# A two-layer convolution block on one core: a split-pool first seam, a second seam with its first image buffer in a pool of its own, and 32x32 products in the tail

## The chip, the core and the metric

The kernel runs on one core of one Trainium2 chip. A core has five engines that work side by side, each with its own queue of instructions: TensorE (PE in the profile, its weight loads PEld), VectorE (DVE), ScalarE (ACT), GpSimd (POOL) and SyncE (SP), which here only issues DMAs. The metric is the time of one execution on the device in microseconds (us). The kernel before takes 3523.01 us, the median of three runs (3522.52 to 3525.32).

## The reference: what is computed

The input x has 16 images of 192 channels and 64x64 pixels, all in float32. Two layers follow each other.

```python
h = _ln2d(x, ln1_w, ln1_b)                        # normalize over the channels
pg = _conv1x1(h, in_proj_w, in_proj_b)            # 192 -> 384 channels
projected, gate = jnp.split(pg, 2, axis=1)
projected = _dwconv3(projected, dw_k)             # 3x3, each channel by itself
scanned = _directional_scan(projected, ...)       # 4 decaying scans, mixed
local = _dwconv3(projected, le_k)
mixed = (scanned + local) * jax.nn.sigmoid(gate)
# batch norm over all images and pixels of a channel, then gelu
x = x + _conv1x1(gelu(bn(mixed)), out_proj_w, out_proj_b)
h2 = _ln2d(x, ln2_w, ln2_b)
x = x + fc2(gelu(fc1(h2)))                        # 192 -> 768 -> 192
# second layer, on the same 16 images
t = relu(scale(x.mean(axis=(2, 3)) @ w1.T))       # 48 numbers for each image
wt = (t @ w2.T + b2) * MASK                       # a 3x3 kernel for each image and channel
out = depthwise_conv(x, wt) + bias                # 4 of the 9 taps are left by the mask
```

The batch norm needs all images before any of them can go on, so the kernel has two seams at which one stage ends and the next begins.

## The kernel before, in words

The kernel has three stages. All orders of instructions are written out by hand (a manual schedule for all five engines): an engine executes its instructions in the order in which the program issues them, and waits for what each needs. Memory comes from pools; a new pool that lies where an old one lay waits for the old one's users.

**Projection** (the start and `project`, L553 to L571). The images are read in 64 chunks (`load_a`, four buffers `xa`). For each chunk, PE turns pixels to partitions (`turn`, L536, tiles xt), DVE takes the moments (`variance`, L543 and L544), ACT the root (`deviation`, L548), and PE multiplies by the weights `wi` (L565, tiles ps_pj). DVE and ACT evict with the scale (L570, L571) into one of two staging tiles: `stg`, or `mid` for odd blocks. Staging is stored to DRAM by groups of 8 channels (`store`, L598, tensors pg_d in five parts); group 0 is kept in SBUF (`store_first`, and for the last block `keep_first`, L591 and L593, after the last eviction). At the start, w_in is loaded into both halves of the partitions (`w0`, in the tile place), scaled by DVE (L310), averaged by PE (L314) and the mean subtracted (L317). Small preparations are hung beside given chunks (`beside`): the vectors from which the convolution matrices are built (loaded as dm and lm), the biases, and the load of the fc1 weights (wf1, wf in the profile) at chunk 62.

**Scans** (`depthwise` to `gate`). Channels are taken in 96 pairs, 4 pairs to a group of 8 channels. For a pair k PE does the 3x3 convolution as products with banded matrices (`depthwise`, L694, ps_d), ACT evicts it to q with three bias operations (L707, L709), DVE does two scans along rows of 1024 elements (L729, L731) with tables of decays made by ACT (L717), PE adds the local convolution (`local`) and the vertical scans (`vertical`), both L738 into ps_l, and DVE multiplies by the gate (L772) and takes the moments for batch norm (L774). The loop (from k=-2) issues vertical(k-1), gate(k-1), scans(k+1), depthwise(k+2), local(k), sigmoid(k). The groups' data arrive by `load_pg` (L681) into three buffers (pg_even, pg_o0, and the first part of mid), 4 MB each, on SP's queue; the products go back to DRAM (mixed_d, L786). Group 1 is loaded in two pieces: its first six images of eight on SP, the last two on POOL after the last block's stores. At k=0, PE also computes hidden_bias (L165) and squeeze_rows (L145); at k=1, 3, 5 ACT scales wf1 (`scale_hidden`, L171).

**The last stage** (`first`, L1080, to the end). After the moments (`class_sums`, `class_moments`, L800 to L808) and `batch_norm` (L812 to L817), images come back in 64 chunks of 512 pixels: DVE transposes (`turn_back`, L276), ACT GELU (`bn_gelu`, L953, L954), PE out projection (`out_proj`, L973 and L980), DVE residual (L986) into image buffers ximg, layer norm (`center` L1021, squares, roots L1046 and L1047), fc1 with GELU (`first`, L1080, L1082), fc2 (`seven`, L925), and onto the image. When a pair of images is complete, `squeeze` computes its taps (L1200 to L1208), and the dynamic convolution of that pair (`dynamic`, L1218 and L66) runs beside the next pair. `idle` and `keep_up` (recorded at L1293 and L823) issue products whose result is not used.

**The tail** (`dynamic_last`, after the loop). The last pair has nothing to run beside. Its 3 tiles of 64 channels (for two images: 128 partitions) have 64 rows each. DVE does tile 0 and 24 rows of tile 1 with four taps (the first on ACT, L1234, three on DVE, L66). PE does tile 2 and 40 rows of tile 1 with the taps on diagonals (`taps_on_diagonals`, L1428) in 64x64 products (L1246), which ACT evicts (L1248) and DMAs store (L1252).

The lines that the tail turns on:

```python
    first_o = room_for(0)
    for r in (0, CR):
        dynamic_last(last, r, CR, 0, None, first_o[:, r:r + CR])
        dynamic_last(last, r, CR, 2, dg2)
    dg1 = taps_on_diagonals(1)
    on_v(1, 1, 0)
    dynamic_last(last, GR, GR, 2, dg2)
```

## Time and profile before

| what | value |
|---|---|
| three runs, median (lowest to highest) | 3523.01 us (3522.52 to 3525.32) |
| the profiled execution, its own time | 3526.05 us |
| its span, first to last instruction | 3524.3 us, 78555 instructions |
| granted clock of PE, mean | 0.998 |
| busy, start (0 to 24 us): PE, DVE, ACT | 24.0 (modelled ends), 14.4, 8.6 us |
| busy, tail (3490 to 3525 us): PE, DVE, ACT | 24.1, 23.7, 14.4 us |
| DMA, whole span | 491.21 MB, mean 139 GB/s |
| DMA, 575 to 599 us | 340 to 418 GB/s in slices of 3 us |

A busy time says how long an engine had an instruction under way; the ends of PE's products are modelled, so that a busy PE is not PE at its peak. A row of the timeline gives the start, the length, the engine, the line, the operation, the tile written and the tile read with their shapes, how many instructions are merged in the row, and in brackets how long the engine sat idle before and what ended that. What ends an idle time is inferred; where the engine named had long been done it was another cause, often a DMA. The chain of waits is followed backward from the last instruction. "PE x128" counts records: each float32 product here has two.

### The profile page before, as it was taken

How to read it: one execution, taken by the hardware profiler on the slowest of the kernel's cores; microseconds unless marked ns; L12 is line 12 of the kernel's file. 1: busy time of each engine (PE TensorE's matmuls, PEld its weight loads, DVE VectorE, ACT ScalarE, POOL GpSimd, SP SyncE). 2: the span in 40 equal slices, each digit the busy share in tenths (PEclk: the TensorE clock that was granted, in tenths of full speed). 3: DMA queues.
4: the chain of work that ended last, by engine and by line, in shares of the span. 5: the costliest groups of instructions: out<-in, count | busy, mean ns of one | idle time of the engine just before them, and what ended most of it. 6: DMA issues, size and time to landing. Idle time of an engine off the chain costs nothing.

```text
span 3524.3 us, 78555 instructions
## 1 busy us (share of the span) xinstructions
PE 3500.5 (99%) x33148; PEld 1982.0 (56%) x33148; DVE 2741.1 (78%) x4666; ACT 1843.7 (52%) x2082; POOL 1177.1 (33%) x1322
## 2 busy tenths in 40 slices
PE   9999999999999999999999999999999999999998
PEld 7869996666666644444444444444444444444443
DVE  7888887999999965567777777777777777767766
ACT  4444446888888843435454544444444445454543
POOL 4545441111111043333343434333333333343433
PEclk9999999999999999999999999999999999999999
DMA  6999999999999941112232222222222222222213
GB/s 186 269 276 283 279 289 300 287 289 284 287 279 283 243 102 42 42 46 70 63 83 58 76 62 80 61 70 67 75 61 70 76 67 71 62 82 58 75 34 91
DMA packets 286505, 491.21 MB, mean 139 GB/s; under 512 B 24720, under 2 KB 180488, under 8 KB 286152
## 3 DMA queue, kind: packets, MB, share of 16 engines
q1 hardware_dynamic: 244100, 340.39, 35.5%
q0 software_dynamic: 41120, 144.77, 14.3%
q8 instruction: 261, 4.28, 0.5%
q10 hardware_dynamic: 932, 1.03, 0.1%
q14 instruction: 92, 0.75, 0.1%
HBM read 284.16 MB, written 197.92 MB: 137 GB/s over the span
## 4 chain that ended last, share of the span: by engine, by line
PE 96%; DVE 2%; DMA 1%; ACT 0%; issue 0%; SPq 0%; ACTq 0%; POOL 0%; DVEq 0%
PE ps_f L1080 28%; PE ps_f L925 19%; PE ps_pj L565 14%; PE ps_l L738 11%; PE ps_s L925 7%; PE ps_d L694 7%; PE ps_o L980 5%; PE ps_o L973 2%; PE ps_xt L536 1%; PE ps_m L1009 1%; PE ps_v L1009 1%; DMA dm<-dv_d 1%; DVE v L731 0%; DVE v L729 0%; DMA mixed_d<-mid 0%; DVE o L66 0%
## 5 line engine op out<-in xcount | busy, mean ns | idle before, releaser
L1080 PE MATMUL ps_f<-h,wf 64*64 64x512 f32 (+1 forms) x9240 | 1014.9, 589 | 0.0
L1082 ACT ACTIVATE gl<-ps_f,bf 128x1024 f32<-128x1024 f32 x384 | 428.2, 1115 | 1076.7 <-PE ps_f L1080 1076.4
L1080 PEld LDWEIGHTS ps_f<-h,wf 64*64 64x64 f32 x9240 | 347.1, 133 | 598.1 <-issue 573.2
L925 PE MATMUL ps_f<-gl,place 128*64 128x256 f32 (+1 forms) x3072 | 528.3, 486 | 1.1 <-ACT rs L1061 1.1
L565 PE MATMUL ps_pj<-wi,xa 64*128 64x384 f32 x3072 | 517.8, 485 | 0.7 <-ACT mid L571 0.4
L565 PEld LDWEIGHTS ps_pj<-wi,xa 64*128 64x128 f32 x3072 | 402.9, 187 | 79.9 <-DVE stg L570 1.7
L1115 POOL TENSOR_TENSOR gl<-gl 128x512 f32<-128x512 f32 x192 | 308.7, 1634 | 159.4 <-PE ps_f L925 159.4
L925 PEld LDWEIGHTS ps_f<-gl,place 128*64 128x64 f32 x3072 | 220.4, 137 | 222.5 <-issue 147.4
L1105 POOL COPY turn<-o 128x1 f32<-128x1 f32 x84 | 16.6, 197 | 820.9 <-DVE o L66 820.9
L1111 POOL TENSOR_TENSOR t<-gl 128x512 f32<-128x512 f32 x192 | 246.4, 1283 | 87.5 <-DVE low L276 44.2
L1113 POOL TENSOR_TENSOR t<-gl,t 128x512 f32<-128x512 f32 x192 | 247.5, 1289 | 43.6 <-ACT gl L1082 30.3
L66 DVE SCALAR_TENSOR_TENSOR o<-ximg,taps,o 128x1024 f32<-128x1024 f32 x180 | 231.7, 1288 | 4.9
L729 DVE TENSOR_TENSOR_SCAN v<-tab,q 128x1024 f32<-128x1024 f32 x96 | 218.3, 2274 | 5.6 <-ACT q L709 5.6
L731 DVE TENSOR_TENSOR_SCAN v<-tab,q 128x1024 f32<-128x1024 f32 x96 | 217.5, 2266 | 0.0
L1138 DVE SCALAR_TENSOR_TENSOR ximg<-ps_f,pt,ximg 128x256 f32<-128x256 f32 (+1 forms) x176 | 96.7, 549 | 145.5 <-PE ps_f L925 145.5
L717 ACT ACTIVATE tab<-mask,dec_b 128x1024 f32<-128x1024 f32 x192 | 209.7, 1145 | 0.1
L523 POOL DMA_DIRECT2D xa<-in_x_dram x201 | 126.1, 634 | 250.4 <-PE ps_pj L565 236.8
L571 ACT ACTIVATE stg<-ps_pj,rsa 128x384 f32<-128x384 f32 x128 | 120.3, 942 | 152.1 <-PE ps_pj L565 140.0
L571 ACT ACTIVATE mid<-ps_pj,rsa 128x384 f32<-128x384 f32 x128 | 119.8, 940 | 152.6 <-PE ps_pj L565 143.5
L986 DVE SCALAR_TENSOR_TENSOR ximg<-ps_o,pt,low 128x256 f32<-128x256 f32 x264 | 112.9, 479 | 94.6 <-PE ps_o L980 90.6
L980 PE MATMUL ps_o<-low,wo 128*64 128x256 f32 x1536 | 180.8, 384 | 1.8 <-ACT low L953 1.8
L276 DVE STREAM_TRANSPOSE low<-low 128x512 f32<-128x512 f32 x180 | 174.4, 1020 | 0.1
(279 smaller groups left out, 5669.8 us busy)
## 6 DMA issues: line engine op xcount, KB each, us to landing
low<-in_x_dram SPq DMA_DIRECT2D x128, 384.0 KB
out_dram<-o SPq DMA_DIRECT2D x172, 256.0 KB
mid<-pg_d SPq DMA_DIRECT2D x8, 4096.0 KB
low<-mixed_d SPq DMA_DIRECT2D x116, 256.0 KB
low<-pg_d SPq DMA_DIRECT2D x7, 4096.0 KB
pg_o<-pg_d SPq DMA_DIRECT2D x7, 4096.0 KB
xa<-in_x_dram POOLq DMA_DIRECT2D x201, 128.0 KB, 5.1
xa<-in_x_dram SPq DMA_DIRECT2D x183, 128.0 KB
```

The costliest lines, as they stand in the source:

```text
L66: nc.vector.scalar_tensor_tensor(o, in0, scalar, in1, ALU.mult, ALU.add, **kw)
L565: nc.tensor.matmul(ps[i], pixels(n, t, g)[q], wi[q, t].rearrange("p g k c -> p (g k c)"), start=(t == 0), stop=(t == 2))
L571: nc.scalar.activation(stag[blk][1][:, :, j], ps[1], AF.Copy, scale=rs[:, g, 1:2])
L694: nc.tensor.matmul(dst(ps[o, ih]), mats[g % 2]["dm"][q, di + 1, :, ch], src(s["pg"][q, :, 0, ch]), start=(di == 0), stop=stop)
L738: nc.tensor.matmul(dst(bst[k]["ps"][o, i]), lm_of(g)[q, m, :, c], src(q, ih), start=start, stop=stop)
L925: nc.tensor.matmul(ps[q], w(i), rhs(i), start=start, stop=stop, **kw)
L980: nc.tensor.matmul(ps[wh][q].rearrange("p (r w) -> p r w", w=32), wo[:, 64 * t:64 * t + 64], cols(rows(s["mx"][:, i]))[:, :, wh], start=fi ...
L1080: nc.tensor.matmul(pf[o, i, x], wf1[q, t, m0:m0 + 64], s["h"][q, t, x], start=(t == 0), stop=(t == 2))
L1082: nc.scalar.activation(gl, pf, AF.Gelu, bias=bf1[:, m:m + 1])
L1111: sub(t1[:, m], b12(m), b11(m))
L1113: sub(t2[:, m], b22(m), t1[:, m])
L1115: sub(b12(m), b22(m), b12(m))
```

## The change

The change has four places. Its parts, in the order of the program:

- **Start.** w_in is loaded into the lower half only, one DMA for each of three parts on SP's and ACT's queues; ACT writes the upper half of wi from it. Chunk 1 of x is loaded on both queues behind a copy of one pixel of chunk 0 (before: chunks 1 to 3 on POOL, behind a copy that needs all of chunk 0). The roots for chunk 0 are taken in two pairs, the reciprocals later.
- **First seam.** The pools are split and ordered so that pg_o0 and q lie over stg alone and ps_d over the banks of xt. The table of pair 0 is made beside chunks 53 and 55, in wf1's room; the idle products are gone; the last block's group 0 is copied in parts, the last rows from PSUM. depthwise(0) is done in two halves of the images, scans(0) in eight pieces. The order at pair 0 is other: depthwise(2) comes after vertical(0). dm(1) is loaded whole; dm(2) is loaded on POOL's queue; the last block's stores go image by image, and pg group 2 is loaded in two pieces.
- **Moved.** hidden_bias goes behind the second class's sums; its addition behind batch norm; squeeze_rows to pair 4; the load of wf1 to pair 88; scale_hidden to the last stage, between the two first GELUs.
- **Second seam.** The first image buffer gets a pool of its own; the first transpose goes between the two moments; the idle product has 256 columns; two transposes for chunk 1 go before the first residual.
- **Tail.** The squeeze of the last pair is done in three parts (tiles 0, 2, 1), with two idle products behind it. DVE does tile 0 only; PE does tiles 1 and 2 in 32x32 products (`dynamic_two`), ACT the first taps, the second diagonals and the evictions, with no DMA on ACT's queue.

The diff, cut to its core:

```diff
-                nc.vector.tensor_scalar_mul(wi[:, t], by_group(w0[:, t]), pt3[:, t, LN1W:LN1W + 1])
+                v, w = by_group(w0[lo, t]), pt3[lo, t, LN1W:LN1W + 1]
+                nc.vector.tensor_scalar_mul(wi[lo, t], v, w)
+                nc.scalar.activation(wi[HALF[1], t], v, AF.Copy, scale=w)
...
+            if n == 1:
+                for q in HALF:
+                    nc.gpsimd.tensor_copy(xa[q, :, 0:1], pixels(0, 1, AR - 1)[HALF[1], 127:128].unsqueeze(1).broadcast_to([64, 3, 1]))
...
+                if n == n_ac - 1 and g == AR - 1:
+                    keep_first(blk, slice(BR - AR, BR - 1))
+                if n == n_ac - 1 and g == AR - 1:
+                    for i, par, q, o in first_of(blk):
+                        if i == 0:
+                            nc.vector.tensor_scalar_mul(o[:, :, j], ps[0][q, 0:2 * GC], rs[q, g, 0:1])
+                        else:
+                            nc.scalar.activation(o[:, :, j], ps[1][q, 0:2 * GC], AF.Copy, scale=rs[q, g, 1:2])
...
-        for _ in range(3):
-            nc.tensor.matmul(warm_[:, 0:2 * C], ident, wi[:, 0].rearrange("p g k c -> p (g k c)"), start=True, stop=True)
-        keep_first(blk)
-        store(blk, 0, (nc.gpsimd, nc.gpsimd))
...
+            for im in (slice(0, n_half // 2), slice(n_half // 2, n_half)) if k == 0 else (slice(0, n_half),):
+                ps = psd.tile([128, 2, CH], F32, tag="d", name="ps_d", bufs=2)
...
         load_pg(1, nc.sync, 0, n_half - 2)
+        store(blk, 0, (nc.gpsimd, nc.sync))
         load_pg(1, nc.gpsimd, n_half - 2, n_half)
-        for d in range(1, len(PARTS)):
-            store(blk, d, (nc.sync, nc.sync))
-        load_pg(2)
+        for i in range(2):
+            for d in range(1, len(PARTS)):
+                store(blk, d, (nc.sync, nc.sync), (i,))
+        load_pg(2, nc.sync, 0, n_half - 2)
+        load_pg(2, nc.sync, n_half - 2, n_half)
...
-                    load_dm(g + 2)
+                    load_dm(g + 2, queues=(nc.gpsimd, nc.gpsimd) if g == 0 else (nc.sync, nc.gpsimd))
...
             if k == 0:
-                pb_h = psb.tile([128, 2, CH], F32, tag="d", name="pb_h", bufs=2)
-                hidden_bias(pb_h)
-                squeeze_rows(pb_h[:, 0, HCH:CH])
-                copy_dm(1)
-            if k in (1, 3, 5):
-                scale_hidden(k // 2)
+                vertical(0)
+                tables(2)
+                depthwise(2)
+            if k == 4:
+                squeeze_rows(psd.tile([128, 2, CH], F32, tag="d", name="pr_h", bufs=2)[:, 0])
+            if k == n_bp - 2 * hp_:
+                load_weights(1)
...
         class_moments(0, pt0)
+        turn_back(y_low, mxs[0], 0, 0)
         keep_up(1)
...
         class_moments(1, pt1)
+        pb_h = psl.tile([128, 2, CH], F32, tag="l", name="pb_h")
+        hidden_bias(pb_h)
         batch_norm()
-        turn_back(y_low, mxs[0], 0, 1)
+        v = bf1.rearrange("p (j i) -> p i j", i=2)
+        nc.vector.tensor_add(v, v, pb_h[:, :, 0:NPS])
         turn_back(y_low, mxs[0], 0, 2)
+        for t in range(2):
+            turn_back(y_low, mxs[1], 1, t)
...
-    slots = [k3.tile([128, 3, GR + 1, RW], F32, tag=f"ximg{i}", name=f"ximg{i}") for i in range(NSL - 2)] + late
+    k4 = ctx.enter_context(tc.tile_pool(name="k4", bufs=1))
+    slots = [(k3 if i else k4).tile([128, 3, GR + 1, RW], F32, tag=f"ximg{i}", name=f"ximg{i}") for i in range(NSL - 2)] + late
...
+        for k in range(NTAP):
+            for u, q in enumerate(QUAD):
+                for j, o in enumerate(QUAD):
+                    r0 = CR * (j % 2) + r + k // 3
+                    nc.tensor.matmul(rows(ps[u][o]), dg[q, k, q], slot(p, g + j // 2)[q, t, r0:r0 + nr, k % 3:k % 3 + HW],
+                                     start=(k == 0), stop=(k == NTAP - 1))
...
+    one(other_taps, 0)
+    dynamic_two(last, 0, 2, dg2, 0, CR // 2, False)
+    one(other_taps, 1)
+    dynamic_two(last, 0, 2, dg2, CR // 2, CR // 2, True)
     dg1 = taps_on_diagonals(1)
+    one(first_tap, 3)
+    one(other_taps, 2)
+    dynamic_two(last, 2, 2, dg2, 0, CR, False)
+    one(first_tap, 4)
+    one(other_taps, 3)
+    dynamic_two(last, 0, 1, dg1, 0, CR, True)
+    one(other_taps, 4)
+    dynamic_two(last, 2, 1, dg1, 0, CR, False)
```

In `dynamic_two`, u is the quarter of the partitions that a product reads (32 channels), j the quarter that it writes (8 or 4 rows of the image). For "apart" the results lie in four banks that ACT evicts one by one, otherwise in two pairs of banks.

## The prediction

> **What bounds the kernel now.** I read the page first, then the windows, then the chain of waits and the timeline at the places where the windows show TensorE short of work.
>
> ```profile
> PE 3500.5 (99%) x33148; PEld 1982.0 (56%) x33148; DVE 2741.1 (78%) x4666; ACT 1843.7 (52%) x2082; POOL 1177.1 (33%) x1322
> PE 96%; DVE 2%; DMA 1%; ACT 0%; issue 0%; SPq 0%; ACTq 0%; POOL 0%; DVEq 0%
> ```
>
> ```profile
> 24.00:560.00 536.00, 535.49 (x4494) 452.20 (x4492) 438.98 (x1344) 239.34 (x318) 234.38 (x443) 1.00 0.93 269
> 700.00:1200.00 500.00, 500.00 (x5813) 331.65 (x5809) 497.46 (x365) 424.00 (x508) 55.59 (x54) 1.00 1.06 284
> 1240.00:1270.00 30.00, 25.19 (x244) 14.23 (x242) 20.31 (x38) 13.67 (x18) 16.79 (x36) 1.00 0.57 146
> 1310.00:3440.00 2130.00, 2130.00 (x19456) 1003.40 (x19452) 1528.29 (x2613) 962.78 (x1000) 794.60 (x701) 1.00 0.24 64
> ```
>
> The columns of the second fence are the stretch, its length, then busy us of PE, PEld, DVE, ACT, POOL, the clock, the DMA share and GB/s. In the three long stretches PE is never short of work, and the change leaves the products there alone. What it touches are four short places: the start (0 to 24 us), the seam between projection and scans (568 to 625), the seam before the last stage (1240 to 1270), and the tail (3487 to 3524). Since PE is full in between, a microsecond won at a place comes out at the end, unless something later was waiting anyway.
>
> **The start: 1.5 us (0.5 to 2.5).**
>
> ```profile
> 1.57 6.34 DMA place<-in_w_in_dram
> ...
> 10.74 1.48 DVE wi L317 x3
> ```
>
> The chain of waits runs from the load of w_in (590 KB, both halves) to 7.91, through DVE's scaling, the mean product and the subtraction, to DVE's first statistics at 12.23; DVE is then the chain until 22.4. The change loads one half (295 KB) in three parts on two queues. At the 245 GB/s that the window from 4 to 6 us shows, 295 KB are 1.2 us; with less queued ahead of the pixels I take the landing at 6.2, 1.7 earlier. ACT makes the other half beside DVE: three copies of 384 elements, some 0.45 each (the 128x1536 square at L1029 takes 1.47 and the fixed part is small), done by 7.7, before the mean product. But the small load ptg is issued one ACT issue (0.7) later; it landed at 8.1, ACT waited 3.6 for it, and DVE's five gain operations (0.17 each) stand before the subtraction. That holds the subtraction to 9.2 or 9.9 instead of 10.74, a gain of 0.8 to 1.5. The reciprocals no longer wait for the root (0.37), and one more of 0.2 stands on the chain. Sum 1.5; ends from ptg late (0.5) to w_in at 5.5 and ptg early (2.5). The gate on one pixel replaces a copy of all (10.59), so x's second chunk starts earlier; behind the gate stand only the loads of later chunks, on POOL and SP.
>
> **The first seam: 3.8 us (2.4 to 6.9).**
>
> ```profile
> 568.73 2.20 PE L658 MATMUL pb<-wi,ident 128*128 128x384 f32 x6
> 569.82 0.84 ACT L593 ACTIVATE low<-mid 64x256 f32<-64x256 f32 x2
> 571.04 8.28 PE L694 MATMUL ps_d<-low,dm 64*64 64x512 f32 x116
> ...
> 575.96 2.29 DVE L729 TENSOR_TENSOR_SCAN v<-tab,q 128x1024 f32<-128x1024 f32 x1 [5.62 <-ACT q L709]
> 579.01 0.93 POOL L681 DMA_DIRECT2D pg_o<-pg_d  x1 [6.94 <-issue]
> ```
>
> ```profile
> 595.71 2.79 PE L694 MATMUL ps_d<-pg_o,dm 64*64 64x512 f32 x40
> ...
> 624.71 2.90 PE L694 MATMUL ps_d<-mid,dm 64*64 64x512 f32 x40 [1.26 <-DMA dm<-dv_d]
> ```
>
> PE fills 2.1 us with idle products until the copies of the last block end at 570.66. In the change the banks of ps_d are those of the pixel transposes, free since 560.9, and the first half of depthwise(0) needs only images 0 to 3, stored long ago: it starts at 568.8. Half a depthwise is ten groups of four products; 512+384+384 columns go at 0.4275 us per four of 512, and four of 120 took 0.119 (from the 2.61 of a whole one), so a half is some 1.5 us. The second half starts at 570.3; the last rows are copied by 569.3 (four POOL copies of 48 elements, COPY of one element 0.20, and small DVE and ACT copies from PSUM). DVE can scan the first half at 571.4 instead of 575.96; its eight short scans are a quarter of 2.27 each, and some 0.06 more. Following PE's new order (depthwise 0, 1, local 0, vertical 0, depthwise 2, 3, local 1, vertical 1) with 2.61 and 4.28 for depthwise and local+vertical, vertical(1) ends at 588.6 instead of 595.7: 7 us less. hidden_bias (2.17), the bias's wait (0.70), copy_dm (1.48 of ACT) and the table of pair 0 have left this stretch; the row product comes back at pair 4 for 0.46 of PE and 0.5 of DVE, which I count within it.
>
> The DMA takes some of it back. Depthwise(4) reads pg group 1, whose last quarter (1 MB, POOL) was issued at 579.01, when the last block's stores had landed, and landed 14.5 later at 593.5, 2.2 ahead of need. In the change two of these stores go on SP behind 3 MB of the group's head. SP waited for the stores from stg until 568.3, then for DVE and for the idle product until 571.0; now only for the first, and wf's 1.2 MB no longer run before it, against 0.4 MB more of dm. Head at 567, done at 576 to 579, the small stores behind it (waiting on SP for the last eviction, 569.8, with the sixteen large ones queued after them; these went at 571.5 before), the quarter issued at 578 to 581 and landed after 13.5 to 14.5: 591.5 to 595. So depthwise(4) starts near 593, a gain of 2.7 where 7 were free. Next is depthwise(8), which waited 1.26 until 624.58 for dm queued behind 4 MB on SP; dm goes to POOL's queue, and pg 2 no longer waits for all stores. 13.2 MB on SP from 567 at 350 to 380 GB/s, with 1.8 MB on POOL, end near 617, due at 593+27.6=620.6. Hence 624.7-620.6=4.1, less 0.3 for the row product: 3.8. With the quarter at 595 it is 2.4, with it in time 6.9. DVE and PE stand at 6.86 and 6.89 us a pair after that, so the lead is kept to the end of the stage.
>
> **The second seam: 1.6 us (0.5 to 2.2).**
>
> ```profile
> 1246.98 1.95 PE L1293 MATMUL ps_i<-wf,ident 128*128 128x512 f32 x4 [1.02 <-DVE mv L808]
> ...
> 1254.18 0.88 DVE L986 SCALAR_TENSOR_TENSOR ximg<-ps_o,pt,low 128x256 f32<-128x256 f32 x2 [3.83 <-PE ps_o L973]
> ```
>
> The chain of waits shows what the label of the last line hides: a store mixed_d<-mid from 1243.57 to 1253.94. The image buffer lies over mid; the product was done near 1252.4. A buffer elsewhere frees 1.8. The idle product of 256 columns is 0.55 shorter, and class_sums(1) follows it. One transpose (1.04) goes into DVE's wait of 1.67 between the moments; another follows the moments as before. So GELU starts at 1248.05 instead of 1249.46. Against it: hidden_bias (2.17 of PE) and its addition end at 1248.15, and the two idle products of the next pool may start only then and run 1.95, so the output product starts at 1250.15, not 1250.75. From there PE goes through without the wait of 1.12 for the residual; centering starts near 1258.4 instead of 1259.98. The three scalings of wf (0.93 each) now stand on ACT before GELU(1), until 1252.9; its last transpose ends at 1255.3, so they cost nothing; without this cover they cost 2.8. The load of wf at pair 88 lies 60 us ahead.
>
> **The tail: 3.2 us (-2 to 6).**
>
> ```profile
> 3490.72 8.59 PE L1246 MATMUL ps_d<-spare,low 64*64 64x256 f32 x96 [2.46 <-issue]
> 3499.12 13.92 PE L1246 MATMUL ps_d<-ximg,low 64*64 64x512 f32 x128
> ...
> 3514.23 1.11 ACT L1248 ACTIVATE ol<-ps_d,pt 128x1024 f32<-128x1024 f32 x1 [3.38 <-DMA out_dram<-ol]
> ...
> 3518.77 0.69 ACT L1248 ACTIVATE ol<-ps_d,pt 128x512 f32<-128x512 f32 x1 [3.42 <-issue]
> ```
>
> ```profile
> 3513.00:3518.00 5.00, 1.77 (x36) 0.97 (x27) 3.34 (x4) 1.11 (x1) 0.00 (x0) 0.96 0.87 259
> ```
>
> DVE's share falls from 88 to 64 rows (15.5 us at 3.88 per 16), PE's rises from 104 to 128, in five calls of 64 products of 32x32, 128 recorded pairs of load and product each, 640 in all. No 32x32 product is in this trace. Below, sixteen side by side would pass 512 columns in the time of four of 64x64: 0.4275/16, 26.7 ns a pair; above, if only four run together, 107 ns. In between, where the columns are few, a pair costs 30 (0.119/4), 33.5 (48 in 1.61 at L155) or 39 ns (24 transposes in 0.93). I take 33.5, the row with the fewest columns and narrow weights: 4.3 us a call. The split squeeze costs DVE 0.65, so PE starts at 3491.2 and ends at 3512.6; ACT needs 2.24 for the last two evictions; from the last eviction's end (3519.46) to the span's end were 4.84. That gives 3519.7. But the stores bind first: 3.15 MB stand behind 3510.6 at 0.298 MB per us (259 GB/s at a share of 0.87), so 3521.2, a gain of 3.2 with rounding. The stall of ACT on its own DMA issues, 3.4 us twice, goes with the scalar queue. Ends: 44 ns a pair gives 3526.3 (-2); 28 ns gives 3518.3 by the bytes (+6). The second idle product keeps the clock, which was 0.56 from 3490.7 to 3494.2; without it PE starts up to 1.7 later.
>
> [...]
>
> **Sum.** 1.5+3.8+1.6+3.2=10.1. The profiled execution has 3526.05 (span 3524.3 and 1.75 around it): 3515.95. The median of the runs is 3.04 below that: 3513.0.
>
> **Rivals.**
> - Forecast, all four near their values: 3513, chance 0.55.
> - The gains fall into other waits: pairs of 40 ns or more in the tail (for it: 39 ns at the transposes), the quarter of pg 1 at 595. 0.8+2.4+1.6+0=4.8, 3518; chance 0.22.
> - The DMA keeps up: pg 1 in time, stores smooth, 2.0+6.5+1.8+5=15.3, 3507.7; chance 0.15. Against it: shares of 1.0 from 575 to 600.
> - Slower: 32x32 products run only four at a time. N of 512 then costs 13.7 a call, 256 6.84: 54.7 instead of 21.4, and the kernel is at 3513.0+33.3, less the 1.5 of backlog that no longer counts: 3544.8. It decides from 40.6 ns a pair in the tail and from 51 ns for the whole kernel. Against it: 64x64 products do run four together here. Chance 0.08.
>
> A measurement tells some 0.2% (7 us) from no change. Faster by more: 0.55+0.15, same 0.22, slower 0.08. The range 3505 to 3521 adds the low ends (1.4) and the high ends (17.6) and leaves the slower rival out.
>
> **What would show it.** Start: first statistics near 10.7. First seam: depthwise at the last projection's end; a PE wait of some 4 us for pg_o near 589; none near 617. Second seam: no residual behind the store; ACT's three wf scalings between the GELUs. Tail: pairs near 33 ns; last DMA within 8 us of the last product. Wrong if PE's 32x32 groups of sixteen take over 0.8 us, or if pg 1 lands after 596.

## The result, and the profile after

The changed kernel takes 3520.07 us (median of 21 runs, 3516.17 to 3524.02), the kernel before 3525.87 beside it (21 runs, 3521.05 to 3533.96). The ratio is 0.9982 with a 95% interval of 0.9976 to 0.9987: **6.3 us faster (4.6 to 8.5)** by the ratio and 5.8 by the two medians, just under the 0.2% that I took as the bound of a difference. The forecast was 10.1 us. The profiled execution has a span of 3518.7 us (before 3524.3).

The busy times and the chain of the page, then the four stretches of the prediction:

```profile
PE 3496.4 (99%) x33570; PEld 1944.7 (55%) x33570; DVE 2736.0 (78%) x4669; ACT 1845.0 (52%) x2097; POOL 1184.1 (34%) x1338
PE 98%; DMA 1%; POOL 0%; SPq 0%; issue 0%; DVE 0%; ACT 0%; POOLq 0%; ACTq 0%
```

```profile
24.00:560.00 536.00, 534.51 (x4492) 358.67 (x4490) 439.77 (x1345) 241.31 (x321) 234.10 (x440) 1.00 0.95 270
700.00:1200.00 500.00, 500.00 (x5810) 380.05 (x5806) 497.47 (x364) 424.67 (x508) 54.95 (x53) 1.00 1.06 284
1240.00:1270.00 30.00, 28.92 (x262) 16.22 (x266) 17.25 (x35) 15.26 (x19) 15.77 (x34) 0.87 0.75 169
1310.00:3440.00 2130.00, 2128.85 (x19436) 1003.14 (x19430) 1529.29 (x2613) 963.96 (x1003) 794.86 (x703) 1.00 0.24 64
```

DVE has left the chain (2% before). The long stretches are as they were. The reader's eye should stop at the third row: PE is busier in the second seam (28.92 us for 25.19) and the clock is 0.87 where it was 1.00. More busy time at a lower clock is no gain.

Four distances split the two executions: to the end of the last gate, from there to the first product of the first fc1, from there to the reduction of the last pool (DVE's `pool<-sums`, the means that the last `squeeze` reads), and from there to the end of the span.

| us | before | after | gain | predicted |
|---|---|---|---|---|
| start and first seam: last gate's end | 1242.27 | 1236.11 | 6.16 | 1.5 + 3.8 |
| second seam: to the first fc1 product | 26.83 | 28.59 | -1.76 | 1.6 |
| last stage: to the pool's reduction | 2218.13 | 2218.13 | 0 | 0 |
| tail: to the end of the span | 37.07 | 35.87 | 1.20 | 3.2 |

**Start and first seam.** DVE's subtraction and first statistics; then the depthwise products, DVE's first scan, POOL's read of the last quarter, and the depthwise products of pairs 4 and 8:

```profile
9.62 1.48 DVE L319 TENSOR_TENSOR wi<-wi,pb 128x384 f32<-128x384 f32 x3 [1.08 <-PE pb L316]
11.02 0.36 DVE L558 BATCH_NORM_STATS2 st<-ps_xt 128x6 f32<-128x192 f32 x1
...
567.36 5.89 PE L724 MATMUL ps_d<-low,dm 64*64 64x256 f32 x114
570.46 4.77 DVE L762 TENSOR_TENSOR_SCAN v<-wf,q 128x256 f32<-128x256 f32 x8 [1.52 <-ACT q L740]
579.43 0.93 POOL L710 DMA_DIRECT2D pg_o<-pg_d  x1 [9.14 <-DMA pg_d<-mid]
590.39 2.91 PE L724 MATMUL ps_d<-pg_o,dm 64*64 64x512 f32 x40 [3.20 <-DMA pg_d<-mid]
618.69 2.80 PE L724 MATMUL ps_d<-mid,dm 64*64 64x512 f32 x40
```

The subtraction stood at 10.74 and depthwise(0) at 571.04. Now depthwise(0) follows the last projection at once, and the scan starts 5.5 us sooner. The bracket at 590.39 (pair 4) shows the new wait that the prediction named: 3.20 us for the last quarter. At pair 8 (618.69) the bracket is gone.

**Second seam.** The bias products (`hidden_bias`, L165, 36 records of one column), the idle pair (L1358, two products whose result is not used), the first output product and the first residual:

```profile
1239.87 4.00 PE L165 MATMUL pb_h<-pt,wf 64*128 64x1 f32 x36
1244.14 3.78 PE L1358 MATMUL ps_i<-place,ident 128*128 128x512 f32 x4 [0.27 <-DVE bf L921]
1247.85 1.12 PE L1024 MATMUL ps_o<-low,wo 128*64 128x256 f32 x8
1249.63 0.88 DVE L1030 SCALAR_TENSOR_TENSOR ximg<-ps_o,pt,low 128x256 f32<-128x256 f32 x2 [2.33 <-PE ps_o L1017]
```

The bias products took 2.17 us in before, where they stood in the first seam:

```profile
582.03 2.17 PE L165 MATMUL pb_h<-pt,wf 64*128 64x1 f32 x36
```

The idle pair took 1.95. Here the two take 4.00 and 3.78. Cut where the granted clock changes, the windows show why (columns as in the prediction, the clock is the third number from the end):

```profile
1234.31:1237.72 3.41, 3.41 (x43) 3.02 (x40) 3.38 (x6) 2.00 (x3) 1.33 (x3) 1.00 0.05 10
1237.72:1241.14 3.42, 3.42 (x28) 3.40 (x30) 2.47 (x8) 0.28 (x1) 0.89 (x1) 0.50 0.79 197
1241.14:1244.55 3.41, 3.14 (x27) 3.06 (x28) 1.50 (x7) 2.53 (x3) 0.00 (x0) 0.50 1.04 296
1244.55:1247.96 3.41, 3.41 (x6) 0.87 (x7) 2.75 (x3) 2.50 (x4) 0.03 (x1) 0.50 0.46 136
```

PE has half the clock for 10.24 us, three stretches of 3.41. Note that PE is "busy" all that time: neither PE's busy time nor a wait in brackets gives it away.

**Tail.** The products of 32x32 squares, the last evictions, and the windows to the end:

```profile
3487.04 4.12 PE L1305 MATMUL ps_d<-spare,low 32*32 32x256 f32 x198 [1.27 <-DVE low L1501]
...
3497.92 4.75 PE L1305 MATMUL ps_d<-spare,low 32*32 32x512 f32 x112
...
3505.64 2.30 PE L1305 MATMUL ps_d<-ximg,low 32*32 32x512 f32 x59 [0.31 <-issue]
3507.89 2.12 ACT L1314 ACTIVATE ol<-ps_d,pt 128x1024 f32<-128x1024 f32 x2 [2.68 <-issue]
```

```profile
3508.00:3511.00 3.00, 0.00 (x0) 0.00 (x0) 0.00 (x0) 2.02 (x2) 1.59 (x3) 1.00 0.91 295
3511.00:3514.00 3.00, 0.00 (x0) 0.00 (x0) 0.00 (x0) 0.00 (x0) 0.54 (x1) 0.50 0.95 253
3514.00:3516.00 2.00, 0.00 (x0) 0.00 (x0) 0.00 (x0) 0.00 (x0) 0.00 (x0) 0.50 0.88 282
3516.00:3518.70 2.70, 0.00 (x0) 0.00 (x0) 0.00 (x0) 0.00 (x0) 0.00 (x0) 0.50 0.17 57
```

198 records in 4.12 us are 20.8 ns a pair of load and product at 256 columns; 112 in 4.75 are 42 at 512. The last eviction ends at 3510.01, 9.4 us sooner than before's (3519.46) on the clock of the span and 5.0 sooner behind the pool's reduction (27.2 us for 32.2), but 8.7 us pass from there to the end, where before had 4.84.

### The profile page after: what moved, and what is told of

It reads as the page before. It is cut to its first block, busy times and chain, and to the rows that moved or that the text cites. A ratio compares the mean times of both kernels' runs of the same rounds, so it can differ in the third digit from the quotient of the medians.

```text
span 3518.7 us, 79438 instructions
## 1 busy us (share of the span) xinstructions
PE 3496.4 (99%) x33570; PEld 1944.7 (55%) x33570; DVE 2736.0 (78%) x4669; ACT 1845.0 (52%) x2097; POOL 1184.1 (34%) x1338
## 4 chain that ended last, share of the span: by engine, by line
PE 98%; DMA 1%; POOL 0%; SPq 0%; issue 0%; DVE 0%; ACT 0%; POOLq 0%; ACTq 0%
PE ps_f L1124 28%; PE ps_f L969 19%; PE ps_pj L580 14%; PE ps_l L768 12%; PE ps_s L969 7%; PE ps_d L724 7%; PE ps_o L1024 5%; PE ps_o L1017 2%; PE ps_xt L551 1%; PE ps_m L1053 1%; PE ps_v L1053 1%; PE ps_d L1305 0%; DMA xa<-in_x_dram 0%; POOL xa L538 0%; SPq L623 0%; DMA pg_d<-mid 0%
## 5 line engine op out<-in xcount | busy, mean ns | idle before, releaser
L762 DVE TENSOR_TENSOR_SCAN v<-tab,q 128x1024 f32<-128x1024 f32 x190 | 423.4, 2270 | 0.3 <-ACT q L740 0.3
L580 PEld LDWEIGHTS ps_pj<-wi,xa 64*128 64x128 f32 x3072 | 308.0, 187 | 170.1 <-DVE stg L593 3.0
L558 DVE BATCH_NORM_STATS2 st<-ps_xt 128x6 f32<-128x192 f32 x512 | 172.1, 336 | 2.8 <-PE ps_xt L551 2.7
```

What stands on the lines that cost most here:

```text
L580: nc.tensor.matmul(ps[i], pixels(n, t, g)[q], wi[q, t].rearrange("p g k c -> p (g k c)"), start=(t == 0), stop=(t == 2))
L762: nc.vector.tensor_tensor_scan(v_, t_, q_, 0.0, ALU.mult, ALU.add)
```

## The experiments

A median of these kernels is sure to some 3 us: all ratios to before below lie between 0.9970 and 0.9987 with intervals that overlap. So the verdicts rest on the distances inside the profiles. Three of them, in us, with the number of 3.41 us stretches at half clock in brackets:

| kernel | depthwise(0) to last gate's end | to the first fc1 product | pool to the end | ratio to before |
|---|---|---|---|---|
| before | 671.2 [1] | 26.83 [0] | 37.07 | 1 |
| e11_before | 670.7 [2] | 28.53 [2] | 37.29 | - |
| after | 668.8 [0] | 28.59 [3] | 35.87 | 0.9982 (0.9976 to 0.9987) |
| e1_idle512 | 670.3 [1] | 27.84 [2] | 34.20 | 0.9983 (0.9975 to 0.9992) |
| e2_hb_early | 673.0 [2] | 24.60 [0] | 35.82 | 0.9987 (0.9978 to 0.9995) |
| e3_stores_pool | 670.5 [1] | 26.04 [1] | 36.11 | 0.9986 (0.9978 to 0.9995) |
| e4_tail_before | 669.1 [1] | 25.96 [1] | 37.30 | 0.9986 (0.9977 to 0.9995) |
| e5_wide_fill | 669.7 [0] | 27.85 [2] | 34.85 | 0.9978 (0.9969 to 0.9986) |
| e6_fewer_bytes | 667.7 [0] | 28.72 [3] | 34.54 | 0.9970 (0.9957 to 0.9983) |
| e7_one_pool | 669.9 [1] | 28.60 [3] | 34.52 | 0.9971 (0.9959 to 0.9982) |
| e8_split_last | 668.7 [0] | 28.59 [3] | 36.35 | 0.9985 (0.9976 to 0.9994) |
| e9_bias_spread | 674.1 [1] | 25.39 [2] | 34.84 | 0.9986 (0.9977 to 0.9995) |
| e10_all | 670.0 [0] | 24.30 [0] | 38.24 | 0.9983 (0.9974 to 0.9991) |
| e12_quiet | 671.3 [2] | 26.25 [1] | 34.37 | - |

In after, e3, e4, e6, e7, e8 and e12 the second seam is the same code (but for e7's pool), and it takes 26.0 to 28.7 us.

### The idle product of 512 columns again

```
-                nc.tensor.matmul(ps[:, 0, 0:HCH], ident, place[:, 0:HCH], start=True, stop=True)
+                nc.tensor.matmul(ps[:, 0], ident, place[:, 0:CH], start=True, stop=True)
```

> The changed kernel with one edit: the idle product at the second seam has 512 columns again (on the small block that the change gave it). In the changed kernel's trace the granted clock falls to 0.50 between 1237.9 and 1247.9 us, after the idle product of 256 columns (0.68 us), while in the trace of before, with 512 columns (1.10 us), it stays at 1.00; the bias products, the two idle products behind them and the way to the first output product then take about 3.5 us more than at the full clock (4.00 for 2.17, 3.78 for 1.95). Theory A, the shorter idle product lets the clock fall: the clock stays at 1.00 through the seam, the bias products take about 2.2 us and the idle pair 1.95, the first output product comes about 9.5 us behind the last gate (12.9 in the changed kernel), and the kernel is 3 to 3.5 us faster than the changed one (about 3517, ratio to before near 0.9973). Rival B, the fall comes from where the stretch of short products lies or from what follows it (the bias products of one column): the clock falls again, the time is that of the changed kernel within 1 us (ratio 0.9982).

The clock fell all the same, 5 us later, for two stretches:

```profile
1236.05:1239.46 3.41, 3.41 (x37) 2.73 (x32) 3.31 (x7) 2.00 (x3) 1.64 (x3) 1.00 0.05 12
1239.46:1242.87 3.41, 3.41 (x49) 3.27 (x48) 2.68 (x6) 0.72 (x2) 0.56 (x1) 1.00 0.87 220
1242.87:1246.29 3.42, 3.16 (x12) 1.83 (x12) 3.01 (x9) 3.16 (x4) 0.00 (x0) 0.50 1.06 302
```

The stretch of the 512 columns kept the clock, the next, with the bias products, lost it. Theory A falls as the only cause. That the bias products bring it down holds for this run; it does not hold for after, where the clock was gone at 1237.72, 2 us before the first of them. What is left of the rival there is where the stretch of short products lies.

### The bias products early

```
+            if k == n_bp - 2:
+                pb_h = psd.tile([128, 2, CH], F32, tag="d", name="pb_h", bufs=2)
+                hidden_bias(pb_h)
...
-        hidden_bias(pb_h)
         batch_norm()
```

> The changed kernel with the 36 bias products and their addition taken out of the second seam and put into the scan stage, behind the last but one channel pair's local products; the idle product keeps its 256 columns. Theory A (the clock falls before the bias products begin, by the short products of the moments and the 256 columns): the clock falls to 0.50 at the same place, the idle pair takes 3.8 us but starts about 4.2 us sooner, the first output product comes at about its earliest, 9.5 us behind the last gate, 3.4 less than in the changed kernel; of this about 2.2 are paid in the scan stage, where PE has no free time, so 1 to 1.5 us faster than the changed kernel (ratio to before near 0.9978). Rival B (the bias products of one column bring the clock down): the clock stays at 1.00 in the seam and the idle pair takes 1.95; the time is the same as under A, the clock tells them apart.

The seam kept its clock with the 256 columns and was the shortest so far, 24.60 us. The clock fell where the bias products had gone, in the middle of the scan stage:

```profile
1226.92:1230.33 3.41, 3.41 (x52) 2.58 (x48) 3.40 (x3) 3.41 (x4) 0.00 (x0) 1.00 0.28 88
1230.33:1233.74 3.41, 3.41 (x20) 1.11 (x20) 2.31 (x3) 1.18 (x2) 0.00 (x0) 0.50 0.32 93
```

Rival B, in this one profile: the bias products at one place bring the clock down, even between local products of 512 columns. They cost 3.1 us there (650.45 us from the products behind the first seam's wait to the last gate, 647.4 in the kernels without them and with the same stretch lost in the first seam), 2.2 of their own; that the rest is the clock's is my reading.

### The small stores on POOL's queue

```
-        store(blk, 0, (nc.gpsimd, nc.sync))
+        store(blk, 0, (nc.gpsimd, nc.gpsimd))
```

> The changed kernel with the small stores of the first seam on POOL's queue alone; in the changed kernel half of them go by SP's queue, behind the large read of the odd rows, and POOL's read of the last quarter waits 9.14 us for them (issued at 579.43, landed near 590.2), so that the depthwise products of the fifth pair wait 3.20 us. Theory A, the order in the queue holds them up: the quarter is issued at 574 to 576, the wait at the depthwise products shrinks to under 1 us, and the kernel is 2 to 3 us faster than the changed one (ratio to before 0.9974 to 0.9976). Rival B, the DMA engines are full in this stretch, so that the quarter lands as late wherever it is queued: wait and time stay within 0.7 us of the changed kernel's.

```profile
576.76 0.93 POOL L710 DMA_DIRECT2D pg_o<-pg_d  x1 [6.43 <-DMA pg_o<-pg_d]
589.41 3.35 PE L724 MATMUL ps_d<-pg_o,dm 64*64 64x512 f32 x28 [3.20 <-DMA pg_d<-mid]
```

POOL's read of the quarter was issued at 576.76, 2.67 us sooner than in after (579.43), of which 0.97 is the earlier start of depthwise(0): 1.70 sooner behind it. TensorE's wait stayed at 3.20 us and ended 23.02 us behind depthwise(0) (23.03 in after). The DMA engines were at 0.92 to 1.09 of their time from 567 to 591 us in both. So rival B, as far as one profile each can tell: in the other kernels with after's queues and the same products in the seam, that wait ended between 21.4 and 24.0 us behind depthwise(0).

### The tail of before

The functions of before's last stage in place of the new ones (the taps in one piece, squares of 64x64, all diagonals on VectorE).

> The changed kernel with the last stage's end of the kernel before: the taps of the last pair in one piece, the products of 64 by 64 squares, no further idle products, all diagonals on VectorE. It gives what the new tail is worth. Theory A, what the two traces show from the reduction of the pool to the end of the span (37.07 us before, 35.87 after): the kernel is 1.2 us slower than the changed one (ratio to before near 0.9986). Rival B, my predicted 3.2 us, of which something else hid 2 in the profiled execution: 3 us slower (ratio 0.9991). Rival C, the clock of 0.56 that the kernel before had in its tail for 3.5 us costs more than the new products gain: no difference.

37.30 us from the pool to the end, as in both profiles of before (37.07, 37.29). The new tail took 34.2 to 36.1 in the seven kernels that have it unchanged and whole, 35.2 in the mean. It is worth 2 us, more than the first pair of profiles shows and less than predicted. The ratio can't tell the three theories apart.

### Wide idle products at both seams

```
+                if k == hp_:
+                    for _ in range(3):
+                        nc.tensor.matmul(ps[:, 0], ident, wide, start=True, stop=True)
...
+            if m % 4 == 0:
+                nc.tensor.matmul(pb[:, 0, HCH:CH], ident, place[:, 0:HCH], start=True, stop=True)
...
-        keep_up(1)
+        keep_up(2)
...
-    idle(2)
+    idle(1)
```

The bias products are 18 products in 36 records, so the edit put two idle products between them, not three.

> The changed kernel with wide idle products where its stages meet. First seam: three of 512 columns on the idle TensorE in front of the fifth pair's depthwise products (the wait there is 1.9 to 3.2 us). Second seam: two of 256 columns for one behind the first moments, one of 256 in front of every 12 of the 36 bias products, and one of 512 for two behind them, so that the seam has about as many wide columns as before, but spread. Theory A, the clock falls for a whole number of stretches of 3.41 us when too few wide columns fall into such a stretch, wherever it begins in that run: the granted clock stays at 1.00 in both seams; from the depthwise products behind the wait to the last gate 645.7 us (647.4 in the runs with a fall there), from the last gate's end to the first product of the first fc1 about 25.5 us (28.6, 27.8, 26.0 and 26.0 in the runs with three, two, one and one stretch), and the kernel is about 2.5 to 3.5 us faster than the changed one (ratio to before 0.9972 to 0.9976). Rival B, the bias products of one column bring it down whatever lies between them: the clock falls in the second seam still, and the gain is at most the first seam's 1.7 us. Rival C, the idle products are themselves on the path and cost what the clock gives: ratio as the changed kernel's, 0.9982.

The first seam kept its clock, but the products stood on the path for what the clock gave back: 669.7 us is no better than the others. In the second seam the clock fell twice, once from the stretch with the products of 48 columns (L155) and once from the one with the bias products and two wide ones:

```profile
1233.55:1236.96 3.41, 3.41 (x51) 3.30 (x48) 3.38 (x6) 2.00 (x3) 1.11 (x3) 1.00 0.02 4
...
1240.37:1243.79 3.42, 3.42 (x40) 2.66 (x40) 2.21 (x8) 2.57 (x3) 0.00 (x0) 1.00 1.03 291
1243.79:1247.20 3.41, 3.15 (x9) 1.26 (x10) 3.05 (x4) 2.06 (x4) 0.07 (x1) 0.50 0.53 155
```

Rival C in the first seam; in the second the clock fell with wide products between the bias products, as B has it. Its ratio's interval includes the changed kernel's ratio.

### Fewer bytes at the end

```
+                if t == 1 and g == 0:
+                    continue
```

> The changed kernel without the eight stores (128 KB each, 1.05 MB of the last pair's 6.29 MB) of the last but one call of the last stage's products; that part of the output is left out. Theory A, the bytes bind the end (the DMA engines are at 0.88 to 0.95 of their time from 3502 to 3516 us, at some 280 GB/s): the last 1.05 MB goes, the end comes sooner by 1.05 MB over 280 GB/s, 3.7 us, as far as the last eviction lets it: from the last eviction's end to the end of the span 5 to 6 us instead of 8.7, from the reduction of the pool to the end 32 to 33 us instead of 34.2 to 36.1. Rival B, what stands behind the last eviction is the time of the last stores themselves (32 partitions each, 4.4 us from issue to landing at the median): the tail stays at 35 us or above.

34.54 us, where A wanted 32 to 33; 7.05 us from the last eviction to the end, where A wanted 5 to 6. A sixth of the bytes (not a twelfth, as the text of e8 below has it), 3.7 us of transfer, brought 0.6 against the mean of 35.2. The way out did get shorter, 7.05 us for 8.6 to 10.4 in the seven kernels with the whole tail (9.2 in the mean), but the last eviction ended later, 27.5 us behind the pool for 25.2 to 27.2 (26.0 in the mean). So the bytes are a part of the way out, and not the bound of the tail alone. A wait grew: TensorE stood for 1.41 us in front of its last products (0.31 in after) and waited for nothing that the profile shows:

```profile
3504.27 2.30 PE L1305 MATMUL ps_d<-ximg,low 32*32 32x512 f32 x59 [1.41 <-issue]
```

### The image buffers in one pool again

```
-    slots = [(k3 if i else k4).tile(...
+    slots = [k3.tile(...
```

> The changed kernel with the image buffers in one pool again, so that the first residual's target lies with the rest. My prediction counted 1.1 to 1.6 us for the second seam, most of it since the residual no longer stands behind the last stores of the scan stage. Theory A, the pool of its own lets the first residual go sooner: the first residual waits for a store of the scan stage in this kernel, and the way from the last gate's end to the first fc1 product is longer by 1 to 2 us at the same number of stretches at half clock (27 to 28 us at one stretch, for 26.0). Rival B, the first output product comes too late for the residual to wait for a store at all (9.1 us and more behind the last gate's end where the clock falls): no difference beyond the stretches at half clock.

28.60 us at three stretches, as 28.59 in after. The first residual started 1.81 us behind the first output product (1.78 in after), and waited for that product. Rival B: the pool of its own is worth nothing in this order of work. Elsewhere it may be worth something: in e10 and e2, whose bias products are out of the seam and whose clock held, the first residual started at 1246.96 and 1249.07, before the scan stage's store that POOL issued landed (1248.27 and 1250.07). Neither was run with one pool. The ratio of 0.9971 comes from six runs and its interval touches the changed kernel's; nothing in its profile makes it faster, so I don't take it for a better version.

### The last call in two

```
-    dynamic_two(last, 2, 1, dg1, 0, CR, False)
+    dynamic_two(last, 2, 1, dg1, 0, CR // 2, False)
+    dynamic_two(last, 2, 1, dg1, CR // 2, CR // 2, True)
```

> The changed kernel with the last call of the last stage's products cut in two calls of 256 columns a square (the first into a pair of banks, the second into four banks apart); the same products and bytes. In the changed kernel 8.7 us pass from the end of the last eviction (1024 columns a partition, 128 KB in each of its four stores) to the end of the span, where before had 4.8, and leaving out a twelfth of the bytes a call earlier brought it to 7.0 only. Theory A, what the last eviction has left to store sets the end: the last eviction ends about as early, with half as much behind it, so 6 to 7 us to the end, and from the reduction of the pool to the end 33 to 34 us (34.2 to 36.1 in the runs so far). Rival B, the DMA engines work off a queue that is full since 3502 us, so that the size of the last piece doesn't matter: 34.2 to 36.1. Rival C, smaller pieces are stored at a lower rate (256 columns are 1 KB a row): slower than 36.

Half right: 6.5 us from the last eviction's end to the end of the span instead of 8.7. But the whole tail took 36.35 us, where the seven kernels with one call took 34.2 to 36.1: rival C's number, though the way out did not get slower. TensorE now stood still twice:

```profile
3503.89 2.79 PE L1305 MATMUL ps_d<-ximg,low 32*32 32x256 f32 x128 [1.25 <-issue]
3509.55 1.62 PE L1305 MATMUL ps_d<-ximg,low 32*32 32x256 f32 x59 [2.87 <-issue]
```

"issue" says that the profile shows nothing that held it. In the DMA records, packets of 16 KB of the queue "instruction" ran from 3501.51 to 3502.43 and from 3507.33 to 3508.29; TensorE went on 1.46 and 1.26 us behind them.

### The bias products spread

```
+            if n_bp - 6 < k < n_bp - 2:
+                m = 2 * (k - n_bp + 5)
+                pb_h = psd.tile([128, 2, CH], F32, tag="d", name="pb_h", bufs=2)
+                hidden_bias(pb_h, (m,))
+                nc.scalar.activation(hb_s[:, m:m + 2], pb_h[:, :, m // 2], AF.Copy)
```

> The changed kernel with the bias products taken out of the second seam and spread over the scan stage, 6 of the 18 behind each of the local products of three of the last pairs, copied by ScalarE and added in the seam. In the runs so far every stretch of 3.41 us at the full clock with 40 or more weight loads and under about 2100 columns (of the whole array) was followed by half clock, and none with 32 loads or fewer; the bias products at one place brought the clock down even in the scan stage, between products of 512 columns. Theory A, it is their density: spread, no stretch of the scan stage falls to half clock, the stage pays about 2.2 us (their time on PE), and from the last gate's end to the first fc1 product it is 24.6 us as with the bias products away altogether; of the two sums (from the depthwise products behind the wait to the first fc1 product) about 672.5 to 674 us, where the changed kernel's seam gave 671.7 at one stretch and 674.3 at three, both without a fall in the first seam. Rival B, any such product does: the clock falls in the scan stage still, 674 to 676.

The scan stage kept its clock with the same products, 12 records to a pair, in this profile and in e10's: it is their density (theory A), as far as two profiles with them spread and one with them together (e2) show. They cost 2.7 us there (650.1 us from the products behind the wait to the last gate, 647.4 with a stretch lost in the first seam and no bias products). The sum that theory A put at 672.5 to 674 us is 675.5 (650.1 and 25.4), the rival's number, but by the second seam: it lost the clock all the same, from a stretch with 40 records of L155:

```profile
1239.08:1242.49 3.41, 3.41 (x50) 3.10 (x46) 3.38 (x6) 2.00 (x3) 1.26 (x3) 1.00 0.06 14
1242.49:1245.91 3.42, 2.46 (x17) 2.28 (x16) 2.31 (x8) 0.05 (x1) 0.95 (x1) 0.50 0.75 193
```

### Three edits together

> Three edits together: the bias products spread as in the run before this, the idle product of 512 columns at the second seam, the last call of the last stage in two. If their effects add up, 1 to 2 us from the second seam and 1 to 2 from the end: about 3 us faster than the changed kernel, ratio to before 0.997 to 0.9975. Rival: the seam's gain is paid in the scan stage and the end is bound by its bytes, ratio 0.998 as the changed kernel.

The one execution whose clock held at 1.00 from 5 us to the end of the products; its second seam is the shortest, 24.30 us. Yet the ratio of 0.9983 is the rival's: 2.9 us were paid in the scan stage, and in the tail TensorE waited 1.40 and 3.40 us for "issue" (38.24 us):

```profile
3503.02 2.81 PE L1308 MATMUL ps_d<-ximg,low 32*32 32x256 f32 x128 [1.40 <-issue]
3509.24 1.46 PE L1308 MATMUL ps_d<-ximg,low 32*32 32x256 f32 x60 [3.40 <-issue]
```

No version of these beats the changed kernel by more than can be told.

### The kernel before, once more

> The kernel before, once more, for a second profile of its seams. Theory A, where the stretches of 3.41 us begin differs from run to run, and with it whether the second seam of before loses one: from its last gate's end to the first fc1 product 26.8 us again if none falls, about 28.5 if one does; the first seam, which has the bias products there, falls to half clock for one stretch again (585.6 us in the first profile). Rival B, the kernel decides and not the run: the same stretches at the same places.

Theory A. One run, 3529.36 us, with half clock in other places than the first profile: two stretches in the first seam, one in the moments, one in the output products:

```profile
1241.29:1244.71 3.42, 3.42 (x61) 3.28 (x55) 3.38 (x5) 1.71 (x3) 0.77 (x2) 1.00 0.00 0
1244.71:1248.12 3.41, 3.41 (x14) 1.91 (x14) 0.93 (x4) 0.28 (x1) 1.45 (x2) 0.50 0.67 173
...
1251.53:1254.95 3.42, 1.61 (x17) 0.69 (x16) 1.65 (x2) 1.94 (x2) 0.00 (x0) 1.00 0.63 183
1254.95:1258.36 3.41, 3.41 (x26) 1.49 (x20) 1.81 (x3) 0.00 (x0) 2.84 (x6) 0.50 0.60 156
```

So the second seam of before, which I read as undisturbed, loses the clock too in other runs.

### The tail with free DMA time

The kernel of two calls without the two stores behind each of VectorE's five pieces (L1288). By the DMA view they are 2.1 MB (6.30 in e8, 4.20 here), not the 2.4 of the text below.

> The kernel of two calls at the end, with the stores of VectorE's rows of the last pair left out (10 stores, 2.4 MB of 6.29; that part of the output is not written), so that the DMA engines have free time in the last stage. In the run with two calls TensorE stands for 1.25 and 2.87 us in front of the last two calls and waits for nothing that the profile shows; a block of 16 KB of instructions (256 of 64 bytes, 128 load and product pairs) goes over the DMA engines each time 1.3 us before it goes on (3507.33 to 3508.29, on at 3509.55). Theory A, TensorE waits for its instructions, whose blocks stand behind the stores in the full DMA queues: with the queues freer the two waits shrink to under 0.5 us each, and the last product ends 2 to 4 us sooner, 25 to 26 us behind the reduction of the pool (28.7 in that run). Rival B, the blocks come at their own pace or TensorE waits for a bank: both waits stay within 0.5 us of 1.25 and 2.87.

Between the two, in one profile.

```profile
3508.95 1.45 PE L1303 MATMUL ps_d<-ximg,low 32*32 32x256 f32 x59 [2.05 <-issue]
```

The wait of 1.25 us was gone, that of 2.87 was 2.05, and the last product ended 27.1 us behind the pool (28.7 with the stores). The packet in front of the remaining wait ran from 3506.07 to 3507.42, when the DMA engines were still at 0.94 of their time; TensorE went on at 3508.95, 1.53 behind it.

## Why the prediction was right, and where it was not

**Start, 1.5 us: right.** The subtraction is 1.12 us sooner and so are the first statistics (12.14 to 11.02 in the timeline), the end of the last projection 1.37 (568.80 to 567.43). That end varies from run to run: 565.9 to 567.7 us in the twelve profiles with the new start, 568.8 and 570.7 in the two of before. (PE's 24.0 us of busy time in the start, in the table ahead of the prediction, is the length of the stretch; the view has 20.73.)

**First seam, 3.8 us: right by its mechanism.** Depthwise(0) at the last projection's end, a wait for the quarter (3.20 where I had some 4), at 590.4 where I had 593, no wait at pair 8. With the start 6.16 us in the first pair of profiles; over the eight profiled executions that have the scan stage unchanged the last gate ends at 1236.6 in the mean, 5.7 before the first profile of before, for 5.3 predicted. The 6.16 has luck in it: before lost a stretch of its clock in this seam (585.60 to 589.01) and after none. At one lost stretch on each side (e1, e3, e4 and e7 against before) the way from depthwise(0) to the last gate's end is 1.3 us shorter (669.9 for 671.2), and with depthwise(0) 2.3 sooner than the start alone makes it, the seam's own gain is some 3.6. That the quarter was bound by where it stood in the queue was wrong in part: issued 1.7 us sooner behind depthwise(0), it landed no sooner (e3).

**Second seam, 1.6 us: wrong.** The failed step is "hidden_bias (2.17 of PE) and its addition end at 1248.15, and the two idle products of the next pool [...] run 1.95". Both durations were rows of a full clock, and I took them to a place where 36 narrow records stand between other narrow ones. I looked for the clock in the tail only. By the windows cut at the clock's changes, the loss is 3 stretches in after; where none falls (e10, e2) the seam takes 24.3 and 24.6 us with the bias products elsewhere, and 26.0 at one stretch with them (e3, e4). Over the seven executions with this code the mean is 27.5, and before has 26.8 with no stretch lost and 28.5 with two: that the row I started from had none was a matter of the run. Whether the gain that I counted is there in work isn't shown, since no profile of this code kept its clock. An estimate of 24.3 us without a fall (26.0 less the 1.7 that a stretch cost in the scan stage) would be 2.5 better than before's 26.8; at two stretches the nearest pair (e1 27.84, e11 28.53) differs by 0.7. The other term, "A buffer elsewhere frees 1.8", measured 0 (e7): the first residual came behind the store's landing in every profile of this code whose landing is recorded (by 0.3 to 3.0 us).

**Tail, 3.2 us: the mechanism right, two terms mis-sized.** "I take 33.5" a pair measured 21 at 256 columns and 42 at 512; in the sum PE ended 20.9 us behind its start (3487.04 to 3507.94) for my 21.4, so this cancelled, by luck: two calls of five at half the price of the other three. "from the last eviction's end (3519.46) to the span's end were 4.84" was taken over from before, whose last piece was half as large; it measured 8.7 here (8.6 to 10.4 in the seven kernels with the whole tail), 6.0 to 6.5 with a last piece of half the size (e8, e12). The bytes that I let bind (3521.2) are no bound of their own (e6): the end is a last piece's eviction and its way out, through engines at 0.9 of their time. Over the seven kernels the last eviction ends 26.0 us behind the pool in the mean, for 32.2 and 32.7 in before, and 9.2 pass from there, for 4.8 and 4.5: most of what the products win goes on the way out, and a gain of 2 is left. The sign "last DMA within 8 us of the last product" failed: 10.8 us (3507.94 to 3518.7). The clock did hold in the new tail: the three profiles of the old one lost a stretch at its start (from 3490.34, 3494.09 and 3483.77), the eleven of the new one none before the last half microsecond of the products. That the second idle product did it wasn't tested (in the stretch that ends at the tail's first products PE was busy for 1.33 of 3.41 us in before, 3486.93 to 3490.34, and for 2.14 in after, 3483.69 to 3487.10). No run shows the second rival's 40 ns as the price of a pair of 32x32 (for it stood the 39 ns of before's transposes): they took 42 at 512 columns and half of that, 21, at 256, and the tail gained 2 us, not 0.

**The range and the rivals.** The range (3505 to 3521) holds 3520.07 with 0.9 us to spare. The forecast of 3513 missed by 7.1: some 4.3 in the gain (5.8 by the medians for 10.1), and 2.9 since the kernel before itself took 3525.87 this time and not the 3523.01 that I started from. By my bound of 0.2% it is the outcome "same", to which I gave 0.22, though the interval (4.6 to 8.5 us) reaches over that bound. The time is nearest to "the gains fall into other waits" (3518) and its tail price, pairs of 40 ns, is what came at 512 columns. Its tail (no gain) and its quarter at 595 (it landed at 590.2) are not, and no wait took the second seam's gain: the clock did. The slower rival's 107 ns a pair is excluded; the DMA did not keep up.

**Open.** What exactly costs the clock. I counted the weight loads and the columns (each record's columns times its share of the 128x128 array) in the stretches from 1226 to 1255 us of all fourteen executions. The 13 that lost the clock by this count have 39 to 55 loads and at most 2042 columns; those with 32 loads or fewer kept it, down to 1032 columns, and so did those with up to 64 loads and 2482 columns or more. One stretch of e11 (1251.53, 16 loads, 2048 columns, PE busy for 1.61 us) fell and breaks this rule. Columns alone, each record counted by its part inside the stretch, do almost as well: those that fell have at most 1465, those that kept the clock 1305 or more, but for one of 1031 (e2). So it isn't shown that the weight loads matter. That the instruction blocks stand behind the stores is supported by six waits that ended 1.26 to 1.53 us behind such a packet, and by e12, which took away half of the waiting and not all; it isn't shown. A tail with free DMA engines throughout wasn't tried.

## What to carry to other kernels

Before a duration is carried to another place, read the granted clock at both, in windows cut at its changes: a busy PE with many narrow products (one column, 48 columns; 39 to 55 weight loads and at most 2042 columns in 3.41 us) lost half its clock in these runs where a wide one (up to 64 loads and 2482 columns or more) kept it. When a seam's time varies from run to run in steps (here 26.0 to 26.3 us at one stretch of half clock, 28.6 to 28.7 at three), profile the kernel, and the one before, more than once before giving the difference to an edit. Small squares buy speed with instructions (here 640 records in 20.9 us for 128 rows, where before had 256 in 24.1 us for 104); where the same DMA engines carry the stores, count the 16 KB blocks too (five in this tail, two in before's).

## What the runs showed of the hardware

- **The clock falls in whole stretches.** Its low times inside the kernels were 3.41, 6.83 and 10.24 us, and all its changes in an execution lie on one grid of 3.413 us (in after from 1237.72 to 3511.00, 2273.28 us, are 666 such steps), whose place differs from run to run (within the grid 2.10 us in after, 0.42 in e1, 1.53 in e2). A low stretch costs about 1.7 us where PE sets the pace (645.7 us against 647.4 from the products behind the first seam's wait to the last gate). In the first seam the seven falls in the changed kernels follow stretches with PE busy for 0 to 1.5 us. It was otherwise in the second seam and in e2's scan stage: of the 14 stretches that lost the clock there, 13 had PE busy for 2.9 to 3.42 us, that is for most or all of the stretch.
- **It comes back after one stretch of wide work.** By the same count, stretches at half clock with 1475 columns or more gave it back, but for one of 1540; those with 778 or fewer did not.
- **Instructions travel by DMA, in blocks.** In the tail five packets of 16 KB on the queue named "instruction" stand in the changed kernel, two in before. The instruction queue in the DMA view, 3484 to 3512 us of after (packets, MB, share of the 16 engines' time):

```profile
q8 instruction: 5, 0.08, 1.2%
```

  and 3488 to 3518 us of before:

```profile
q8 instruction: 2, 0.03, 0.5%
```

  In the long last stage (1310 to 3440 us) of after there are 152, one every 14 us, 2.49 MB for 38866 loads and products of TensorE: 256 to a packet, or 64 bytes each. In the tail one comes every 4.4 to 5.5 us, beside stores: in stretches of 2 to 3.5 us from 3490.5 to 3511 us the DMA engines are at 0.76 to 0.94 of their time.
- **A pass of sixteen 32x32 squares** (one record of load and product for each; a float32 product has two such passes: 128 records to a call of 64 products) took 0.33 us at 256 columns and 0.67 at 512 in after.
